# Edge scores as a maximum and a minimum: W1's columns sorted by the sign of W2, self loops as items of the edge stage

## The chip, the core and the metric

The kernel runs on one core of a Trainium2 chip. The metric is device time in microseconds (us), from start to end of one execution. The engines named below are TensorE (PE, matrix products), VectorE (DVE, elementwise), ScalarE (ACT, elementwise with a function and an optional sum), GpSimd (POOL, here mostly the issuer of indirect DMAs) and SyncE (SP, which issues plain DMAs). Each engine runs its own queue in order and waits for the others by semaphores.

## What is computed

Four graph layers are applied to 32 entries of 512 nodes with 256 features. Layers 0 and 3 are of one kind and hold the costly part:

```python
pre_u = jnp.einsum('bud,dk->buk', h_t, W1[:d])
pre_v = jnp.einsum('bvd,dk->bvk', h_t, W1[d:])
hidden = jax.nn.relu(pre_u[:, :, None, :] + pre_v[:, None, :, :] + b1)
S = jax.nn.sigmoid(jnp.einsum('buvk,ko->buvo', hidden, W2)[..., 0] + b2[0])
a_t = jnp.einsum('buv,bud->bvd', S * A_a, h_t)
m_t = jnp.einsum('uv,bud->bvd', A_m, h_t) * h_t
z_t = beta1 * h_t + beta2 * (a_t @ Wa + ba) + beta3 * (m_t @ Wm + bm)   # per entry
```

`A_a` and `A_m` are both the adjacency `adj` (512 x 512), which is nonzero at about 1.6% of its places and on the whole diagonal. The score `S` is therefore needed only where `adj` has an edge. Layer 1 is `z + relu(adj z W^T + b)`; layer 2 is an attention whose logits are `f1[i] + f1[j]`, with a leaky relu, plus `adj`, and a softmax over all 512 nodes.

## The kernel before

**Lists of edges.** `Counts` (L177) counts on the chip how many edges each node has. Eight places per node (`OWN`) are filled from its own edges; what is over goes into four "panels" of 128 lines. If there are more than fit, the register `excess` sends the program into `dense_path`; else `sparse_path` runs. With four blocks of 128 nodes the 32 own items and 4 panels make `ITEMS` = 36 items: an item holds one edge for each of 128 partitions. `Edges.build` makes the indices: `iv` (the row to fetch for the other end), `iu` (for the panels, the row of the first end) and `cell` (where the score goes).

**Groups.** Four entries (`NB`) form a group; there are eight groups, and each passes layer 0 (`g0`) and layer 3 (`g3`), so sixteen edge stages run. `pre` (L583) makes, for each entry of a group and each block of 128 nodes, the products with both halves of W1, adds b1 to the first (L596, DVE), copies the second (L597, ACT), and writes both to a table in HBM (`table`, L604, SP). It also makes the score of the node with itself (L599, L600).

**The edge stage** is `edges` (L649). For each item it fetches 128 rows of the table by an indirect DMA on POOL (L646), 1024 wide (four entries of 256), and adds the first end, `mine` (L731, DVE). `mine` is a plain load on SP (L692) for own items and a gather for the panels. Then relu times W2, summed over 256: in half of the steps, and in all steps of the first and of the last group (`spare`), one 1024-wide DVE instruction (L739) and four summing ACT instructions (L717); in the others four DVE instructions of 256 with an accumulator (L747). Every four items an exponential (L614, ACT), two DVE operations (L618, L619) and a product with the edge's value (L675) make the scores, and POOL scatters them into a dense matrix in HBM (`put`, L639). The scores of the self loops go through the same operations as `own` (`own_1`, L666), at the second and fourth step, and are written to the diagonal by SP (L670). A gather is issued `lead` steps ahead, 3 or, at the ends, 5.

**The rest.** `load` (L772, POOL) brings the finished matrix back as `SA`, once all of the group's puts have landed. `middle_one` does layers 0 to 2 of one entry on PE, with a softmax in between on ACT and DVE (L958 to L964), whose result PE transposes (L1003), and then `pre` for layer 3. `last` does layer 3 of a group.

**The order of the work.** `weave` merges the streams by times written out by hand in units of one group's middle stage (`sparse_path`, L1159 on); a stream is a generator, and each `yield` ends a piece. The middle stages of the groups follow each other; edge stages, the `first` and the `last` of neighbouring groups run beside them. `edge_times` spreads an edge stage's steps over its stretch. The setup, the first group's `pre` and its edge stage come before the first middle stage; the last group's edge stage comes after the last one, beside `last` of the group before, and its own `last_behind` ends the program.

Of the kernel before, what the change touches and what calls it, by code (L numbers as in the profile page):

```python
# [31 lines left out]
LEAD = 3  # L32
LEAD_AT_ENDS = 5
TAIL = 6
EARLY = 20
CELLS = HALF * N
ITEMS = NC * OWN + 2 * PANELS
SPARE = NC // 2 * OWN * P + LINES
GROUP = NB * D
HELD = 12  # L40


def mm(nc, out, pairs):
# [5 lines left out]
class Model:  # L49


    def __init__(self, ctx, tc, a):
        nc = self.nc = tc.nc
        self.tc, self.a = tc, a
        const = self.const = ctx.enter_context(tc.tile_pool(name="const", bufs=1))
        self.ident = const.tile([P, P], F32, name="ident")
        make_identity(nc, self.ident)
        self.adj = const.tile([P, NC, N], F32, name="adj")
        for c in range(NC):
            nc.sync.dma_start(self.adj[:, c, :], a["adj"][c * P : (c + 1) * P, :])  # L60
        self.g0, self.g3 = self.gnn_first("L0_gnn"), self.gnn_first("L3_gnn")

    def rest(self, temp, psum):
# [34 lines left out]
    def gnn_first(self, L):  # L98
        nc, a, const = self.nc, self.a, self.const
        w = {"L": L}  # L100
        w["W1"] = self.load(f"{L}_W1", [P, 2 * DC, D], a[f"{L}_W1"].rearrange("(c p) k -> p c k", p=P))
        w["b1bc"] = self.bcast(f"{L}_b1", D)
        w["W2bc"] = const.tile([P, D], F32, name=f"{L}_W2bc")
        nc.scalar.dma_start(w["W2bc"], a[f"{L}_W2"].rearrange("k o -> (k o)").partition_broadcast(P))
        w["b2"] = self.bcast(f"{L}_b2", 1)
        w["nb2"] = const.tile([P, 1], F32, name=f"{L}_nb2")
        w["bcol"] = const.tile([P, DC, 1], F32, name=f"{L}_bcol")
        if L == "L3_gnn":
            w["bbc"] = const.tile([P, D], F32, name=f"{L}_bbc")
        for key in ("Wa", "Wm"):  # L110
            w[key] = const.tile([P, DC, D], F32, name=f"{L}_{key}")
        return w
# [64 lines left out]
class Counts:  # L177
# [3 lines left out]
    def __init__(self, ctx, m):  # L181
# [4 lines left out]
        with tc.tile_pool(name="c_sb", bufs=2) as sb, tc.tile_pool(name="c_ps", bufs=1, space=PSUM) as ps:  # L186
            ones = sb.tile([P, N], F32, name="c_ones", bufs=1)
            nc.vector.memset(ones, 1.0)
            count = sb.tile([P, NC], F32, name="count", bufs=1)
            there = sb.tile([P, NC], F32, name="c_there", bufs=1)  # L190
            for c in range(NC):
# [13 lines left out]
            nc.tensor.matmul(pc, ones[:, 0:1], self.lines, start=True, stop=True)  # L205
            half = sb.tile([1, 2], F32, name="half")
            nc.vector.tensor_reduce(half, pc.rearrange("p (h c) -> p h c", h=2), AX.X, ALU.add)
            most = sb.tile([1, 1], F32, name="most")
            nc.vector.tensor_reduce(most, half, AX.X, ALU.max)
            nc.vector.tensor_scalar(self.excess, most, float(-LINES), None, ALU.add)  # L210


def item_of(c, k):
# [190 lines left out]
class Group:  # L404
# [3 lines left out]
    def __init__(self, sp, w, name):  # L408
        self.w = w
        self.table = sp.dram.tile([2 * N, GROUP], F32, name=f"table_{name}")  # L410
        self.cells = sp.cells[name[0]]
        self.layer = name[0]
        self.puts = [f"puts_{name}_{q}" for q in range(2)]
        self.written = [[], []]
        self.s = sp.grp.tile([P, ITEMS, NB], F32, name=f"s{name[0]}")
        self.self_s = sp.grp.tile([P, NC, NB], F32, name=f"self_s{name[0]}")


def by_two(t, n=2):
# [3 lines left out]
class Sparse:  # L423
# [98 lines left out]

    def big(self, dtype, n, layer=None):

        self.bigs += 1
        if layer is None:
            layer = 3 if self.bigs <= NC else 0
        return self.act.tile([P, n], dtype, name="big", tag=f"SA{layer}", bufs=NC)

    def setup(self):  # L530


        for w in (self.m.g0, self.m.g3):
            self.nc.vector.tensor_scalar(w["nb2"], w["b2"], -1.0, None, ALU.mult)
        self.zero = self.act.tile([P, GROUP], F32, name="zero", tag="hWa3")
        self.nc.gpsimd.memset(self.zero, 0.0)

        edges = self.built = self.e.build(self.counts, self.adjT, self.lists, self.psum, self.big, self.act)
        for _ in range(NC):
            next(edges)  # L540
            yield
        self.rest = self.m.rest(self.big(F32, 2048), self.psum)
        next(self.rest)
        self.zeros("0")
        yield
        for _ in range(NC + 2 * (OWN // 2 + 1)):
            next(edges)
            yield
# [16 lines left out]

    def setup_rest(self):
        yield from self.rest

# [11 lines left out]
    def pre(self, g, b, hT):  # L582
# [3 lines left out]
        for c in range(NC):  # L586
            cs = slice(c * P, (c + 1) * P)
            if c % 2 == 0:
# [4 lines left out]
            pp = two[c % 2]  # L593
            nc.tensor.matmul(pp, hT[:, 1, cs], w["W1"][:, 1::DC, :], start=False, stop=True)  # L594
            puv = self.small.tile([P, 2, D], F32, name="puv", bufs=3)
            nc.vector.tensor_tensor(puv[:, 0, :], pp[:, 0:D], w["b1bc"], ALU.add)  # L596
            nc.scalar.copy(puv[:, 1, :], pp[:, D:])  # L597
            both = self.small.tile([P, D], F32, name="both", bufs=1)
            nc.vector.tensor_tensor(both, pp[:, D:], puv[:, 0, :], ALU.add)  # L599
            nc.vector.scalar_tensor_tensor(  # L600
                both, both, 0.0, w["W2bc"], ALU.max, ALU.mult, accum_out=g.self_s[:, c, b : b + 1]
            )
            self.settle()
            self.later = lambda c=c, puv=puv: nc.sync.dma_start(rows[:, c, :, b, :], puv)  # L604
            yield
# [44 lines left out]
    def edges(self, g, spare=(), own_tags=()):  # L650
# [11 lines left out]

        def own_1():
            self.sigmoid_of(own)
            diag = self.counts.diag.unsqueeze(2).to_broadcast([P, NC, NB])
            nc.vector.tensor_tensor(g.self_s, g.self_s, diag, ALU.mult)  # L666
            for q in range(2):
                diagonal = g.cells[q][q * HALF : q * HALF + HALF * (N + 1), :]
                diagonal = diagonal.rearrange("(c p a) b -> p c a b", p=P, a=N + 1)[:, :, 0, :]
                self.written(g, q, nc.sync.dma_start(diagonal, g.self_s[:, 2 * q : 2 * q + 2, :]))  # L670

        def run_1(ks):
            self.sigmoid_of(g.s[:, ks, :].rearrange(flat))
# [4 lines left out]
                ready.append((e.half_of(j), e.cell[:, j : j + 1], g.s[:, k, :]))  # L678

        panels = [j for j in e.order if j >= NC * OWN][: len(own_tags)]  # L680

        def fetch(n):
            if n == EARLY:
                for j, tag in zip(panels, own_tags):
                    mine[-j] = self.act.tile([P, GROUP], F32, name="mine_more", tag=tag)
                    self.fetch(mine[-j], g, e.iu[:, j - NC * OWN : j - NC * OWN + 1])
            j = e.order[n]
            c = -j if -j in mine and j >= NC * OWN else j // OWN
            if c not in mine:
                t = self.gath.tile([P, GROUP], F32, name="mine", bufs=3)  # L690
                if c < NC:
# [7 lines left out]
                rows = self.act.tile([P, GROUP], F32, name="rows_more", tag=tag)  # L699
            else:  # L700
                rows = self.gath.tile([P, GROUP], F32, name="rows")
            self.fetch(rows, g, e.iv[:, j : j + 1])
            fetched[n] = rows, t

        def put():
# [4 lines left out]
                self.half = r[0]  # L710
                self.put(g, *r)

        def sums(k, rows):

            for b in range(NB):
                part = rows[:, b * D : (b + 1) * D]
                self.behind(nc.scalar.activation(part, part, AF.Identity, accum_out=g.s[:, k, b : b + 1]))  # L717

        summed = []
        self.half = 1  # L720
# [1 line left out]
            fetch(n)  # L722
            yield

        todo = [(2, lambda: self.exp_of(w, own)), (4, own_1)]
        done = 0
        for k in range(ITEMS):
            for _ in range(2 if spare and len(ready) > 2 else 1):
                put()
            rows, other = fetched.pop(k)  # L730
            self.behind(nc.vector.tensor_tensor(rows, rows, other, ALU.add))  # L731
            if k + lead < ITEMS:
                fetch(k + lead)
            if summed:
                summed.pop(0)()
            if spare or k % 2 == 1 and k < ITEMS - 3:
                by_entry = rows.rearrange("p (b d) -> p b d", b=NB)
                w2 = w["W2bc"].unsqueeze(1).to_broadcast([P, NB, D])
                nc.vector.scalar_tensor_tensor(by_entry, by_entry, 0.0, w2, ALU.max, ALU.mult)  # L739
                summed.append(lambda k=k, rows=rows: sums(k, rows))  # L740
                if spare:
                    summed.pop(0)()
            else:
                for b in range(NB):
                    part = rows[:, b * D : (b + 1) * D]
                    at = g.s[:, k, b : b + 1]
                    nc.vector.scalar_tensor_tensor(part, part, 0.0, w["W2bc"], ALU.max, ALU.mult, accum_out=at)  # L747
            if k % 4 == 3 or k >= ITEMS - 3:
                ks = slice(done, k + 1)
                near = spare or k >= ITEMS - 5  # L750
                todo.append((k + (1 if near else 3), lambda ks=ks: self.exp_of(w, g.s[:, ks, :].rearrange(flat))))
                todo.append((k + (1 if near else 4), lambda ks=ks: run_1(ks)))
                done = k + 1
            while todo and todo[0][0] <= k:
                todo.pop(0)[1]()
            yield
        for _, f in todo:
# [380 lines left out]

def edge_times(ahead, a, b, behind, lead=LEAD):

    step = (b - a) / ITEMS
    first = [ahead + j * min(step, (a - ahead) / lead) for j in range(lead)]
    return first + spread(even(ITEMS), a, b) + spread(even(TAIL), b, behind)


def middle_shares(given):
# [15 lines left out]
def sparse_path(ctx, m, counts, xr, outr, B):  # L1162
# [4 lines left out]
    streams = [  # L1167
        (sp.setup(), spread(even(NC + 1 + NC + 2 * (OWN // 2 + 1) + 1), -0.40, -0.295), ""),
        (sp.setup_behind(), spread(even(2 * (OWN // 2 + 1) + 2 * PANELS + 4), -0.285, -0.16), ""),
        (sp.setup_rest(), spread(even(7), -0.26, -0.20), ""),  # L1170
        (sp.zeros_behind(), spread(even(2), 0.15, 0.2), ""),
    ]
    for t in range(last + 1):
# [276 lines left out]
```

## Time and profile before

| what | value |
|---|---|
| median of the runs | 2977.59 us (2975.59 to 2987.02, 3 runs) |
| the profiled execution, its own time | 2998.45 us |
| its span | 2996.8 us |
| granted PE clock, mean | 0.959 |
| moved by DMA | 677.30 MB |
| first group's edge stage: first add, last add | 90 us, 223 us |
| first load of SA | 229 us |
| last group's edge stage: first add, last add | 2834 us, 2946 us |

Busy times are of one profiled execution. A row of a group of instructions gives line, engine, operation, what it writes from what, shapes, how often; then its busy time in us and the mean duration of one in ns; then the idle time of the engine just before it and what ended most of that. A row of waits gives who waited for what: us in total, times, the longest. A row of windows gives a stretch in us, its length, and the busy us of PE, of PE's weight loads, of DVE, ACT and POOL, each with its number of instructions, then the granted PE clock, the busy share of the DMA engines and GB/s. In the summary the digits are tenths of busy time in 40 equal slices of the span.

### The profile page before, as it was taken

To read this page: it belongs to the slowest core of one execution; us is meant where nothing else is said; L and a number is where in the kernel's file an instruction comes from. 1 tells how busy PE (TensorE), PEld (TensorE's weight loads), DVE (VectorE), ACT (ScalarE), POOL (GpSimd) and SP (SyncE) were. 2 spreads that over 40 slices of the span, in tenths; PEclk is the share of its full clock that TensorE was granted. 3 is DMA by queue.
4 is the path that set the end of the run, shared out by engine and by line. 5 is a ranking of instruction groups with operands and counts; after the bars stand their busy time and mean duration, and the time that the engine had idled before them with its cause. 6 is when DMAs were issued, how large, how long until landed. Compare 5 with 4: busy or idle time off the path is not lost. (4 is left out here: it accounts for less than half of the span.)

```text
span 2996.8 us, 32453 instructions
## 1 busy us (share of the span) xinstructions
PE 2690.0 (90%) x8645; PEld 1613.9 (54%) x8646; DVE 2307.1 (77%) x6035; ACT 1336.8 (45%) x4101; POOL 1555.3 (52%) x1328
## 2 busy tenths in 40 slices
PE   6367787989998999989999899989999899988998
PEld 3134344545664566546664466646565466644666
DVE  6874786889588885988778885888858896783494
ACT  3553454445344443544344443445434453453262
POOL 2662463646445673556536464466735564361183
PEclk9678998999999999999999999999999999999999
DMA  8875657796678867787677866687677866663474
GB/s 268 286 225 169 213 174 221 233 300 203 217 217 269 268 211 227 230 262 254 209 222 247 275 207 230 216 268 253 211 228 236 303 227 197 208 211 102 148 244 150
DMA packets 302143, 677.30 MB, mean 226 GB/s; under 512 B 52608, under 2 KB 170880, under 8 KB 293760
## 3 DMA queue, kind: packets, MB, share of 16 engines
q0 software_dynamic: 122688, 414.40, 42.9%
q1 hardware_dynamic: 160304, 223.52, 23.0%
q10 hardware_dynamic: 18960, 37.24, 3.4%
q8 instruction: 70, 1.15, 0.2%
q14 instruction: 121, 0.99, 0.1%
HBM read 529.02 MB, written 146.01 MB: 225 GB/s over the span
## 5 line engine op out<-in xcount | busy, mean ns | idle before, releaser
L646 POOL DMA_INDIRECT rows<-table,iv x552 | 679.0, 1230 | 795.5 <-DMA table<-puv 262.7
L639 POOL DMA_INDIRECT cells<-s,cell x576 | 697.6, 1211 | 420.6 <-DVE s L675 243.2
L731 DVE TENSOR_TENSOR rows<-rows,mine 128x1024 f32<-128x1024 f32 x552 | 666.4, 1215 | 101.4 <-DMA rows<-table,iv 72.8
L717 ACT ACTIVATE rows<-rows 128x256 f32<-128x256 f32 x1088 | 439.6, 406 | 445.4 <-DVE rows L739 396.6
L46 PE MATMUL pst<-adj,h 128*128 128x512 f32 x1024 | 452.2, 592 | 0.0
L747 DVE SCALAR_TENSOR_TENSOR rows<-rows,L_gnn_W2bc 128x256 f32<-128x256 f32 x1120 | 414.0, 417 | 1.6
L739 DVE SCALAR_TENSOR_TENSOR rows<-rows,L_gnn_W2bc 128x1024 f32<-128x1024 f32 x272 | 329.4, 1213 | 0.4
L46 PEld LDWEIGHTS pst<-adj,h 128*128 128x128 f32 x1024 | 192.8, 190 | 219.9 <-issue 217.6
L46 PE MATMUL pst<-L_gnn_Wa,hT 128*128 128x256 f32 x1024 | 248.8, 393 | 62.9 <-DMA hT<-xT 57.8
L46 PEld LDWEIGHTS pst<-L_gnn_Wa,hT 128*128 128x128 f32 x1024 | 198.9, 199 | 103.0 <-issue 59.2
L46 PE MATMUL pst<-eT,feats 128*128 128x512 f32 x512 | 237.7, 619 | 10.9 <-ACT eT L1004 10.9
L46 PE MATMUL pst<-adjT,zW 128*128 128x512 f32 x512 | 228.2, 599 | 11.6 <-ACT zW L916 9.7
L596 DVE TENSOR_TENSOR puv<-pst,bc_L_gnn_b 128x256 f32<-128x256 f32 x256 | 104.9, 416 | 162.4 <-DMA table<-puv 89.2
L597 ACT COPY puv<-pst 128x256 f32<-128x256 f32 x256 | 93.2, 371 | 288.1 <-DVE puv L596 225.9
L1061 PE MATMUL pst<-hWa,SA 128*128 128x256 f32 x896 | 220.3, 400 | 0.0
L1061 PEld LDWEIGHTS pst<-hWa,SA 128*128 128x128 f32 x896 | 213.8, 328 | 3.7 <-issue 1.7
L717 ACT ACTIVATION_READ_ACCUMULATOR rows<-rows 128x1 f32 x1088 | 204.7, 188 | 0.0
L860 ACT COPY flat<-SA 128x512 f32<-128x512 f32 x128 | 136.7, 1128 | 136.6 <-issue 62.9
L891 PE MATMUL pst<-flat,hWa 128*128 128x512 f32 x448 | 196.8, 592 | 0.0
L592 PE MATMUL pst<-w_L_gnn_W,hT 128*128 128x512 f32 x256 | 141.5, 681 | 53.9 <-ACT hT L579 36.5
L46 PEld LDWEIGHTS pst<-eT,feats 128*128 128x128 f32 x512 | 99.9, 198 | 133.2 <-issue 113.3
L46 PEld LDWEIGHTS pst<-adjT,zW 128*128 128x128 f32 x512 | 96.5, 191 | 133.4 <-issue 114.0
(176 smaller groups left out, 3984.2 us busy)
## 6 DMA issues: line engine op xcount, KB each, us to landing
table<-puv SPq DMA_DIRECT2D x256, 256.0 KB
SA<-cells POOLq DMA_DIRECT2D x64, 1024.0 KB
h<-in_x_dram SPq DMA_DIRECT2D x64, 512.0 KB
mine<-table SPq DMA_DIRECT2D x64, 512.0 KB
hT<-xT SPq DMA_DIRECT2D x36, 512.0 KB
xT<-hT ACTq DMA_DIRECT2D x32, 512.0 KB
x2T<-yT SPq DMA_DIRECT2D x32, 512.0 KB
x2s<-x ACTq DMA_DIRECT2D x64, 256.0 KB
```

The source lines that it names most:

```text
L46: nc.tensor.matmul(out, lhsT, rhs, start=(n == 0), stop=(n == len(pairs) - 1))
L592: nc.tensor.matmul(pp, hT[:, 0, ks], w["W1"][:, 0::DC, :], start=True, stop=False)
L596: nc.vector.tensor_tensor(puv[:, 0, :], pp[:, 0:D], w["b1bc"], ALU.add)
L639: ins = self.nc.gpsimd.indirect_dma_start(out=g.cells[half], out_offset=bass.IndirectOffsetOnAxis(ap=at, axis=0), in_=s, in_offset=None)
L646: self.nc.gpsimd.indirect_dma_start(out=rows, out_offset=None, in_=g.table, in_offset=bass.IndirectOffsetOnAxis(ap=at, axis=0))
L717: self.behind(nc.scalar.activation(part, part, AF.Identity, accum_out=g.s[:, k, b : b + 1]))
L731: self.behind(nc.vector.tensor_tensor(rows, rows, other, ALU.add))
L739: nc.vector.scalar_tensor_tensor(by_entry, by_entry, 0.0, w2, ALU.max, ALU.mult)
L747: nc.vector.scalar_tensor_tensor(part, part, 0.0, w["W2bc"], ALU.max, ALU.mult, accum_out=at)
L860: self.nc.scalar.copy(flat[:, r, :], SA[r][:, :, b])
L891: nc.tensor.matmul(pz, hWa[:, r, cs], flat[:, r, :], start=(r == 0), stop=False)
L1061: self.nc.tensor.matmul(pz[:, k * D : (k + 1) * D], SA[r][:, cs, b], hWa[:, r, :], start=(r + k == 0), stop=(alone and k == 1 and r == NC ...
```

## The change

For a column with weight w, `w * relu(u + v)` equals `max(w v, -w u) + w u` if w is positive and `min(w v, -w u) + w u` if it is negative. So if the tables hold `w v` and `-w u`, an edge needs one maximum over the positive columns, one minimum over the negative ones, a sum, and the subtraction of the sum of the first end's row, which belongs to the node and not to the edge.

- **Ranks** (`ranks`, called in `Counts` ahead of the counting): from W2 as a column the place of each column is made: 112 positive ones first (`SURE`), 112 negative ones next, and the 32 left over (`MIXED`) last. If a sign has fewer than 112 columns, `excess` becomes positive.
- **Sorted W1** (`sorted_W1`, once a layer in the setup): W1 is transposed on PE and multiplied by matrices that hold one scaled entry per column, which sorts and scales it in one product; the same for b1 and W2. The two broadcast loads a layer (b1, W2) are replaced by two loads as columns.
- **`pre`**: L599 and L600 are gone. L596 is split: 224 columns with an accumulator (the sum per node, `less`), and 32 without.
- **`edges`**: 40 steps in place of 36: the four self loops are steps too (`seq`, negative numbers), each with a plain load of its rows on SP, and sums always on ACT. Each step: maximum (4 x 112), minimum (4 x 112), addition (4 x 32), and relu times W2 on 4 x 32. A panel also subtracts its first end, 4 x 224. The sums are on ACT as before, or one DVE reduction over 4 x 256 in place of four accumulating instructions. `less` is subtracted before the exponential: by `own_less` for the self loops, by `less(ks)` for the items. `own_1` runs four steps behind the last self loop. `EARLY` goes from 20 to 24.

```diff
-EARLY = 20
+EARLY = 24
+STEPS = ITEMS + NC
+SURE = 112
+MIXED = D - 2 * SURE
+PLACE = {0: 0, 2: 1, 1: 2, 3: 3}
...
+        nc.scalar.dma_start(w["W2col"], a[f"{L}_W2"].rearrange("(c p) o -> p c o", p=P))
         w["W1"] = self.load(f"{L}_W1", [P, 2 * DC, D], a[f"{L}_W1"].rearrange("(c p) k -> p c k", p=P))
-        w["b1bc"] = self.bcast(f"{L}_b1", D)
-        nc.scalar.dma_start(w["W2bc"], a[f"{L}_W2"].rearrange("k o -> (k o)").partition_broadcast(P))
+        nc.scalar.dma_start(w["b1col"], a[f"{L}_b1"].rearrange("(c p o) -> p c o", p=P, o=1))
...
             nc.vector.memset(ones, 1.0)
+            signs = self.ranks(m, sb, ps, ones)
...
+    def sorted_W1(self, w):
+        nc = self.nc
+        t = self.big(F32, 2048, 0)
+        W1T = t[:, 0 : 2 * N].rearrange("p (c d) -> p c d", c=DC)
+        by_v, by_u = (t[:, k * N : (k + 1) * N].rearrange("p (c d) -> p c d", c=DC) for k in (2, 3))
+        for to, scale in ((by_u, w["su"]), (by_v, w["sv"])):
+            for c in range(DC):
+                nc.vector.tensor_scalar(
+                    to[:, c, :], self.m.upto_D, w["place"][:, c, :], scale[:, c, :], ALU.is_equal, ALU.mult
+                )
+        for c in range(DC):
+            pt = self.psum()
+            for r in range(2 * DC):
+                nc.tensor.transpose(pt[:, r * P : (r + 1) * P], w["W1"][:, r, c * P : (c + 1) * P], self.m.ident)
+            nc.scalar.copy(W1T[:, c, :], pt)
+        for k, to in enumerate((by_u, by_v)):
+            pp = self.psum()
+            for d in range(DC):
+                rs = slice((DC * k + d) * P, (DC * k + d + 1) * P)
+                mm(nc, pp[:, d * D : (d + 1) * D], [(W1T[:, c, rs], to[:, c, :]) for c in range(DC)])
+            nc.scalar.copy(w["W1"][:, DC * k : DC * (k + 1), :], by_two(pp))
...
-            nc.vector.tensor_tensor(puv[:, 0, :], pp[:, 0:D], w["b1bc"], ALU.add)
+            sure = slice(0, 2 * SURE)
+            less = g.less[:, PLACE[c], b : b + 1]
+            nc.vector.scalar_tensor_tensor(
+                puv[:, 0, sure], pp[:, sure], 1.0, w["b1bc"][:, sure], ALU.mult, ALU.add, accum_out=less
+            )
+            nc.vector.tensor_tensor(puv[:, 0, 2 * SURE :], pp[:, 2 * SURE : D], w["b1bc"][:, 2 * SURE :], ALU.add)
             nc.scalar.copy(puv[:, 1, :], pp[:, D:])
-            both = self.small.tile([P, D], F32, name="both", bufs=1)
-            nc.vector.tensor_tensor(both, pp[:, D:], puv[:, 0, :], ALU.add)
-            nc.vector.scalar_tensor_tensor(
-                both, both, 0.0, w["W2bc"], ALU.max, ALU.mult, accum_out=g.self_s[:, c, b : b + 1]
-            )
...
+            if k < 0:
+                nc.sync.dma_start(rows, places[c, 1])
+            else:
+                self.fetch(rows, g, e.iv[:, j : j + 1])
...
-        todo = [(2, lambda: self.exp_of(w, own)), (4, own_1)]
+        todo = [(last_own + 3, own_less), (last_own + 4, own_1)]
...
-            self.behind(nc.vector.tensor_tensor(rows, rows, other, ALU.add))
+            self.behind(nc.vector.tensor_tensor(rows[:, :, ups], rows[:, :, ups], other[:, :, ups], ALU.max))
...
+            nc.vector.tensor_tensor(rows[:, :, downs], rows[:, :, downs], other[:, :, downs], ALU.min)
+            nc.vector.tensor_tensor(rows[:, :, mixed], rows[:, :, mixed], other[:, :, mixed], ALU.add)
+            nc.vector.scalar_tensor_tensor(rows[:, :, mixed], rows[:, :, mixed], 0.0, w2, ALU.max, ALU.mult)
+            if k >= 0 and e.order[k] >= NC * OWN:
+                sure = slice(0, 2 * SURE)
+                nc.vector.tensor_tensor(rows[:, :, sure], rows[:, :, sure], other[:, :, sure], ALU.subtract)
+            to = g.s[:, k, :] if k >= 0 else g.self_s[:, PLACE[-1 - k], :]
-            if spare or k % 2 == 1 and k < ITEMS - 3:
+            if spare or k < 0 or k % 2 == 1 and k < ITEMS - 3:
...
-                for b in range(NB):
-                    part = rows[:, b * D : (b + 1) * D]
-                    at = g.s[:, k, b : b + 1]
-                    nc.vector.scalar_tensor_tensor(part, part, 0.0, w["W2bc"], ALU.max, ALU.mult, accum_out=at)
+                nc.vector.tensor_reduce(to, rows, AX.X, ALU.add)
```

## The prediction

> **What bounds the kernel now.** I read the summary and the slices first, then the waits of TensorE, then windows over the two ends, then the groups.
>
> ```profile
> PE 2690.0 (90%) x8645; PEld 1613.9 (54%) x8646; DVE 2307.1 (77%) x6035; ACT 1336.8 (45%) x4101; POOL 1555.3 (52%) x1328
> ...
> PE   6367787989998999989999899989999899988998
> ...
> DVE  6874786889588885988778885888858896783494
> ```
>
> TensorE (PE) is the bound in the middle, but not at the left end: the first four slices have it at 6, 3, 6, 7 tenths, while VectorE (DVE) is at 6 to 8. PE idles 307 us in all. Its waits:
>
> ```profile
> PE pst L46 <- DMA hT<-xT: 57.8, 4, 25.7
> PE pst L1003 <- DVE ex L964: 51.7, 27, 10.8
> ...
> PE pst L1003 <- DVE cols L963: 29.3, 8, 6.3
> ```
>
> The first row is four waits before 236 us. The other two, 81 us, are the softmax of the middle stage (L958 to L964), held up because DVE has edge work queued before it. The start and the tail by windows:
>
> ```profile
> 90.00:110.00 20.00, 4.09 (x8) 2.44 (x9) 18.67 (x40) 9.47 (x43) 10.76 (x9) 0.50 0.95 367
> 110.00:130.00 20.00, 12.17 (x29) 4.90 (x27) 20.00 (x49) 15.75 (x61) 15.68 (x11) 0.91 0.72 237
> 130.00:150.00 20.00, 0.00 (x0) 0.00 (x0) 20.00 (x47) 9.32 (x44) 14.72 (x12) 0.51 0.70 213
> 150.00:170.00 20.00, 16.52 (x48) 9.66 (x48) 20.00 (x40) 14.30 (x61) 14.60 (x13) 0.89 0.72 216
> ...
> 2834.00:2890.00 56.00, 52.45 (x196) 41.66 (x196) 55.97 (x68) 33.72 (x154) 39.75 (x30) 0.97 0.79 283
> 2890.00:2955.00 65.00, 56.95 (x176) 35.32 (x175) 53.68 (x76) 35.96 (x159) 52.18 (x42) 0.92 0.63 206
> ```
>
> Columns after the length: PE, PE loads, DVE, ACT, POOL. From 90 to 170 us DVE is full (78.7 of 80): this is the first group's edge stage, which must end before the first middle stage may start (its L772 loads run at 229 to 240). From 2834 to 2955, the last group's edge stage, DVE, PE and, with its 0.3 us between DMAs, POOL all have little room. The chain of waits says the same: PE up to 2818, then DVE (L731, L739), then PE.
>
> **The change, part by part.** The rows to price it:
>
> ```profile
> L731 DVE TENSOR_TENSOR rows<-rows,mine 128x1024 f32<-128x1024 f32 x552 | 666.4, 1215 | 101.4 <-DMA rows<-table,iv 72.8
> L717 ACT ACTIVATE rows<-rows 128x256 f32<-128x256 f32 x1088 | 439.6, 406 | 445.4 <-DVE rows L739 396.6
> L747 DVE SCALAR_TENSOR_TENSOR rows<-rows,L_gnn_W2bc 128x256 f32<-128x256 f32 x1120 | 414.0, 417 | 1.6
> L739 DVE SCALAR_TENSOR_TENSOR rows<-rows,L_gnn_W2bc 128x1024 f32<-128x1024 f32 x272 | 329.4, 1213 | 0.4
> L599 DVE TENSOR_TENSOR both<-pst,puv 128x256 f32<-128x256 f32 x256 | 107.3, 419 | 30.7 <-ACT puv L597 21.5 <-ACT flat L860 0.6 <-issue 0.4
> L600 DVE SCALAR_TENSOR_TENSOR both<-both,L_gnn_W2bc 128x256 f32<-128x256 f32 x256 | 107.3, 419 | 2.8
> ```
>
> 256 elements take 0.417 us and 1024 take 1.215, so an instruction costs 0.15 us and 1.04 ns an element. That prices 448 elements (4 x 112) at 0.617, 128 at 0.284, 224 at 0.384, 32 at 0.184, 896 at 1.08. They overlap a little: in the timeline, two independent 1024-wide adds take 2.35 us together. I therefore take 0.07 off each unless the next needs its result.
>
> (a) A step whose sums ACT makes: before, 1.21 + 1.14 = 2.35. After, max 0.54, min 0.54, add 0.28, L739's form 0.21, together 1.57. Saved 0.78.
> (b) A step whose sums DVE makes: before, 1.21 + 4 x 0.42 (L747 with its accumulator read) = 2.89. After, 1.64 and one reduction over 1024. No row shows that reduction; at the bottom it is a 256-wide instruction (0.42), at the top the four accumulating ones (1.68); the nearest row is a 1024-wide pass, 1.14 to 1.21, and I take 1.14: 2.78, saved 0.11.
> (c) Four more steps a group for the self loops, kind (a): 1.57 each. A panel step also subtracts 896 elements, 1.01. The subtractions of `less`, some 11 a group at 128x16, have L675's 0.168, or 0.1 overlapped.
> (d) In `pre`, L599 and L600 go and L596 splits into 224 wide with an accumulator and 32 wide: 1.14 becomes 0.50, 16 times a group: 10.2 saved.
>
> A normal group has 16 steps (a) and 20 (b): 95.4 before; after, 20 x 1.57 + 20 x 2.78 + 4.0 + 1.1 = 92.1; with (d) 13.5 saved. In the first and the last group all steps are (a): 84.6 before, 40 x 1.57 + 5.1 = 67.9 after; with (d) 26.9. All sixteen: 14 x 13.5 + 2 x 26.9 = 243 us of DVE. Without the overlap it is 91; these are the two ends.
>
> A rule speaks against this. The Trainium skill, "VectorE: DVE Perf Modes", The DRAIN you can't avoid, says that each operation is followed by a flush of about its duration less 266 ns, before which the next doesn't start, so that op count should be kept low; its Rules for kernel authors call tensor_reduce the slowest operation, at 1x. By that flush step (a) would go from 4.3 to 2.5 us; but then two 1024-wide adds would need over 3 us to the second's end, and they take 2.35, so the row decides: no flush, 0.78 saved. The 1x is what L731 and L739 already run at, so the reduction gets no surcharge. What remains of the op-count rule is the 0.15 us each, counted above.
>
> (e) ACT: 64 self steps x 4 sums x 0.41 (start to start in the timeline) = 105 us more, on an engine 45% busy: hidden. Without that cover it is 6.6 us a group.
> (f) DMA: 64 plain loads of 512 KB, 34 MB on 677; POOL gets no new instruction. They go on SP's queue and wait there for a `rows` buffer; behind them stand the next `table` writes and the hT and h loads. Costed at nothing because the `mine` loads (L692, also 64 on SP, also issued a lead ahead) never appear as what DVE waited for. Two broadcasts of 128 KB a layer go, two columns come.
> (g) `own_1` moves from step 4 to about step 29 of 40, with its exponential, three 128x16 DVE operations and two SP DMAs of 4 KB. It passes the hT, `mine` and `table` entries of SP; SPq L670 already waits 73.8 us in all. The loads of SA wait for it, but the puts of the last items are later; without those, some 10 steps of slack are left.
> (h) Start, before the branch: `ranks` stands ahead of the counts on DVE and needs the column of L3's W2, fifth on ACT's DMA queue. ACT issued its fifth at 5.2 us; landed at about 7.5, then some 30 small operations at 0.1 to 0.17 and three short PE hops, done at 12; then 2.8 + 0.9 + 1.6 for the counts: 17 against 12.2. **+5**, ends +2 (a landing before 5) and +9 (behind both W1 loads).
> (i) Sorting W1 of L0: 8 transposes (2.2 us at L173's 1.09 per four), 12 matmuls of 256 columns (2.7, at 16 in 3.62), four copies of 0.58, 2.2 us of DVE. Some 8 us in series; the landing of x hides it for the first `pre` (x is issued at 13.0, its transposes start at 21.1), but it stands ahead of the edge lists on DVE and PE: **+3**, ends 0 and +8. L3's sort adds 2.2 us of DVE to 90 to 170.
>
> **The sum**, on the profiled run (span 2996.8 us, its own time 2998.45; the median of the runs is 0.7% less):
> - 0 to 90: +5 +3, and 16 x 0.64 = 10.2 saved in `pre`, of which I count 4, since 30 to 50 us is held by DMA (share 1.01, DVE half idle): +4.
> - 90 to 236: in the full 80 us stand 22 steps, three self steps to come and 10 `pre`: -17.2 + 4.7 - 6.4 + 2.2 = -16.7. Behind 170 DVE waits for PE; I count -2. About -19.
> - 236 to 660: PE waits 38 us before L1003 (summed over the timeline's gaps there); DVE loses 40 x 0.64 + 2 x 3.3 = 32 of some 330. I count -15.
> - 660 to 2640: 32 us of such waits, mostly 1 to 2 us each, which is the latency of the chain: -6. To 2730: 10 us of them: -2.
> - Tail: DVE would give 17, but PE is busy 109 of 121 us there: -7.
> Sum -45: 2953.5, and scaled by the 0.7%, **2933 us**.
>
> **Rivals.**
> 1. **SP turns into a stall** (slower). A self fetch waits on SP for a row buffer. POOL's same wait took 105.9 + 102.5 us in 101 cases, 2.1 us each, longest 26. If SP holds 2.1 us and half reaches PE through late hT or `table`, 64 x 1.05 = +67: 2999. It decides from 0.7 us of PE time per fetch (45 / 64). For it: PE's 57.8 us on hT. Against: `mine`.
> 2. **Hidden.** PE is the bound, the start's cost eats the start's gain, and only the tail gives 7: 2970. For it: 98% PE at 1000 to 1170. Against: DVE full from 90 to 170.
> 3. **More than forecast.** The softmax waits nearly vanish (-60 in place of -23) and the start gives 10 more: 2886.
> 4. The transform does not do what it says: a sign count outside 112 to 144 takes the dense path. The reference's seed gives W2 133 positive values of 256 in both layers (the keys are the same), so both 112s are filled: left out.
>
> **Chances.** Forecast 0.48 (its own range 2905 to 2960), more 0.15, hidden 0.17, SP 0.20. Range for 8 in 10: 2886 to 3000, from the third rival to the first. The runs before spread 0.38%, so 0.5%, 15 us, is about what can be told from no change. Faster by over that: 0.48 + 0.15 and a little of the hidden case, 0.65; within 0.15; slower 0.20.
>
> **What would show it.** DVE busy 2070 to 2215; ACT near 1440; max and min rows at 0.6 us; the reduction at 1.2; first instruction behind the branch at 18 in place of 13; the first SA load some 15 us earlier; the L1003 waits about 55. The forecast is wrong if SP's waits for `rows` come with PE waits on hT or DVE waits on `rows` from `table`, or if DVE waits for ACT's sums at `less`.

## The result, and the profile after

The changed kernel takes 3412.07 us (median; 3405.46 to 3423.3) against 2980.4 in the same session: a ratio of 1.145, with a 95% interval of 1.1407 to 1.1494. Forecast was 2933, with 2886 to 3000 as the range. The time lies far outside it, on the slow side.

The busy times of the page after:

```profile
span 3404.5 us, 33200 instructions
...
PE 2814.4 (83%) x8720; PEld 1679.0 (49%) x8720; DVE 2134.9 (63%) x5789; ACT 1434.6 (42%) x4621; POOL 1364.6 (40%) x1332
...
PE   7567787789978899778987899878997889978978
...
DVE  6745657677466766666576675667746676574363
```

VectorE (DVE) did become lighter, 2135 us in place of 2307, and ACT reached 1435: both as forecast. But no engine is full any more. TensorE (PE) idles 590 us (span less busy) in place of 307, and for nearly the same number of instructions it is busy 124 us longer, at a granted clock of 0.922 in place of 0.959. These two, 283 and 124, are the whole 408 us between the spans.

The loss is spread over the middle. From 800 to 1150 us (columns as in the windows of before):

```profile
800.00:1150.00 350.00, 296.97 (x913) 176.38 (x912) 223.76 (x590) 134.97 (x428) 140.03 (x136) 0.93 0.67 216
```

PE was busy 333.82 of these 350 us before, at a clock of 0.99. The start is not where it went: the first loads of SA run at 210 to 220 us, 19 us sooner than before.

What DVE waits for, in the rows of the costliest groups:

```profile
L867 DVE TENSOR_TENSOR rows<-rows,mine 128x448 f32<-128x448 f32 x608 | 376.1, 619 | 597.2 <-DMA rows<-table,iv 464.9
L862 DVE TENSOR_TENSOR rows<-rows,mine 128x448 f32<-128x448 f32 x608 | 371.0, 616 | 189.4 <-DMA rows<-table,iv 123.4
...
L880 DVE TENSOR_REDUCE s<-rows 128x4 f32<-128x1024 f32 x280 | 336.7, 1204 | 0.5
```

L862 is the maximum, L867 the minimum, L880 the reduction. Each takes what was forecast: 0.617 us for 448 elements, 1.2 for the reduction. New is the idle time: DVE stood 597 us in front of the minimum and 189 in front of the maximum; before, 101 in front of the one addition (L731). In the kernel text the maximum of an item comes first. So its minimum should never have to wait for the gathered rows: they have landed when the maximum starts. It waits because it does not stand behind it. In the compiled list of DVE's instructions the minimum precedes the maximum of its own item in 447 of 640 cases.

In the timeline (start, length, instruction, idle before it and its releaser):

```profile
1532.68 1.21 DVE L880 TENSOR_REDUCE s<-rows 128x4 f32<-128x1024 f32 x1
1533.81 0.27 DVE L869 SCALAR_TENSOR_TENSOR rows<-rows,L_gnn_W2bc 128x128 f32<-128x128 f32 x1
1539.26 0.63 DVE L867 TENSOR_TENSOR rows<-rows,mine 128x448 f32<-128x448 f32 x1 [5.17 <-DMA rows<-table,iv]
1539.80 0.28 DVE L868 TENSOR_TENSOR rows<-rows,mine 128x128 f32<-128x128 f32 x1
1540.12 0.29 DVE L869 SCALAR_TENSOR_TENSOR rows<-rows,L_gnn_W2bc 128x128 f32<-128x128 f32 x1
1540.33 0.68 DVE L940 TENSOR_TENSOR mhT<-pst,hT 128x512 f32<-128x512 f32 x1
```

A minimum stands 5.17 us at the head of DVE's queue for its gather. Behind it stands L940, a product of the middle stage that feeds PE's matmuls. The waits of PE show the same end of it; L1038, L1062 and L1120 are DVE work of the middle stage, and L669 is an ACT copy ahead of `pre`. After, then the like rows of before:

```profile
PE pst L682 <- ACT hT L669: 120.6, 17, 14.9
PE pst L1051 <- DVE hT L1038: 82.2, 22, 11.1
PE pst L1073 <- DVE yT L1062: 52.8, 28, 5.4
...
PE pst L682 <- DVE yT L1120: 35.6, 11, 5.5
```

```profile
PE pst L592 <- ACT hT L579: 36.5, 11, 4.9
...
PE pst L934 <- DVE yT L923: 11.2, 14, 1.6
...
PE pst L912 <- DVE hT L899: 8.2, 6, 2.3
```

### The profile page after: what moved, and what is told of

Its sections match the earlier page's. It is cut to its first block, busy times and chain, and to the rows that moved or that the text cites. A ratio compares the mean times of both kernels' runs of the same rounds, so it can differ in the third digit from the quotient of the medians.

```text
span 3404.5 us, 33200 instructions
## 1 busy us (share of the span) xinstructions
PE 2814.4 (83%) x8720; PEld 1679.0 (49%) x8720; DVE 2134.9 (63%) x5789; ACT 1434.6 (42%) x4621; POOL 1364.6 (40%) x1332
## 5 line engine op out<-in xcount | busy, mean ns | idle before, releaser
L736 POOL DMA_INDIRECT rows<-table,iv x548 | 581.0, 1060 | 1298.3 <-ACT rows L846 298.1
L846 ACT ACTIVATE rows<-rows 128x256 f32<-128x256 f32 x1320 | 532.4, 406 | 544.2 <-DVE rows L862 321.1
L867 DVE TENSOR_TENSOR rows<-rows,mine 128x448 f32<-128x448 f32 x608 | 376.1, 619 | 597.2 <-DMA rows<-table,iv 464.9
L729 POOL DMA_INDIRECT cells<-s,cell x576 | 615.8, 1069 | 295.4 <-issue 139.1
L862 DVE TENSOR_TENSOR rows<-rows,mine 128x448 f32<-128x448 f32 x608 | 371.0, 616 | 189.4 <-DMA rows<-table,iv 123.4
L880 DVE TENSOR_REDUCE s<-rows 128x4 f32<-128x1024 f32 x280 | 336.7, 1204 | 0.5
L846 ACT ACTIVATION_READ_ACCUMULATOR rows<-rows 128x1 f32 x1320 | 249.9, 189 | 5.2 <-issue 5.2
L1051 PE MATMUL pst<-WT,hT 128*128 128x256 f32 x512 | 153.6, 465 | 91.4 <-DVE hT L1038 82.2
L1073 PE MATMUL pst<-WT,yT 128*128 128x257 f32 x512 | 137.5, 418 | 60.9 <-DVE yT L1062 52.8
L1051 PEld LDWEIGHTS pst<-WT,hT 128*128 128x128 f32 x512 | 120.1, 239 | 134.0 <-DVE hT L1038 78.6
L688 DVE SCALAR_TENSOR_TENSOR puv<-pst,L_gnn_b1bc 128x224 f32<-128x224 f32 x256 | 98.4, 384 | 132.1 <-PE pst L684 75.0
```

The costliest lines, as they stand in the source:

```text
L729: ins = self.nc.gpsimd.indirect_dma_start(out=g.cells[half], out_offset=bass.IndirectOffsetOnAxis(ap=at, axis=0), in_=s, in_offset=None)
L736: self.nc.gpsimd.indirect_dma_start(out=rows, out_offset=None, in_=g.table, in_offset=bass.IndirectOffsetOnAxis(ap=at, axis=0))
L862: self.behind(nc.vector.tensor_tensor(rows[:, :, ups], rows[:, :, ups], other[:, :, ups], ALU.max))
L867: nc.vector.tensor_tensor(rows[:, :, downs], rows[:, :, downs], other[:, :, downs], ALU.min)
L880: nc.vector.tensor_reduce(to, rows, AX.X, ALU.add)
L1051: nc.tensor.matmul(pw[:, at], zT[:, d, cs], m.WT_1[:, d, :], start=(d + k == 0), stop=(d * k == 1))
```

## The experiments

**Why would the minimum run ahead?** The text of a kernel here is not its final order: the instructions are scheduled anew per engine, and what depends on nothing may be moved forward. `behind` adds an order that carries no data: an instruction of an edge stage may not come before a mark of the middle stage. The kernel before wrapped its one addition in it, and everything else in the step used the addition's result. The change wraps the maximum alone. Minimum and mixed addition write other columns, so neither depends on the maximum.

Three theories were put against each other: this one of the **order**; **SP**, whose queue holds the middle's loads behind the self fetches; and the **lead**, gathers issued too late for 40 denser steps.

```diff
-            nc.vector.tensor_tensor(rows[:, :, downs], rows[:, :, downs], other[:, :, downs], ALU.min)
-            nc.vector.tensor_tensor(rows[:, :, mixed], rows[:, :, mixed], other[:, :, mixed], ALU.add)
+            self.behind(nc.vector.tensor_tensor(rows[:, :, downs], rows[:, :, downs], other[:, :, downs], ALU.min))
+            self.behind(nc.vector.tensor_tensor(rows[:, :, mixed], rows[:, :, mixed], other[:, :, mixed], ALU.add))
```

> The minimum and the addition of the mixed columns are also ordered behind the middle stage, as the maximum is. Order theory (the minimum, which nothing orders, stands in DVE's queue in front of the maximum of its own item and waits there for the gather): DVE's waits on rows from the table fall from about 660 us to under 200, PE idles about 300 us in place of 585, time 2920 to 2990. SP theory (the self fetches on SP's queue hold the loads of the middle stage): time stays above 3300. Lead theory (the gathers are issued too late for the shorter steps): time stays above 3300.

Measured: 3041.78 us, ratio to before 1.0192 (1.0152 to 1.0231). Two changed lines take back 370 of the 432 us, where the other two theories had the time above 3300. DVE's waits on `rows` are down to 168 us and PE's idle time to 327, of which the copy at L669 has 35.7. No minimum stands in front of its maximum any more, and the rows say so:

```profile
L862 DVE TENSOR_TENSOR rows<-rows,mine 128x448 f32<-128x448 f32 x608 | 376.1, 619 | 194.7 <-DMA rows<-table,iv 151.3 <-issue 17.2 <-DMA rows<-table 13.8
L867 DVE TENSOR_TENSOR rows<-rows,mine 128x448 f32<-128x448 f32 x608 | 371.5, 611 | 0.0
```

The wait at the minimum is gone, not moved: the maximum's is what it was. But the time is above the expected 2990, so something else is left.

Then the same fault alone, put into the kernel before: the addition cut in three, with the second and third piece free, or held.

```diff
-            self.behind(nc.vector.tensor_tensor(rows, rows, other, ALU.add))
+            self.behind(nc.vector.tensor_tensor(to[0], to[0], by[0], ALU.add))
...
+            for i in (1, 2):
+                nc.vector.tensor_tensor(to[i], to[i], by[i], ALU.add)
```

> The kernel before, with its addition of 1024 cut into 112, 112 and 32 columns of each entry; only the first piece is ordered behind the middle stage. Nothing else of the change. Order theory: slower by 4 to 14%, 3100 to 3400, with DVE waiting for rows at the free pieces. SP theory and lead theory: only the two more DVE instructions a step count, about 0.15 us each, 576 times: 0 to 3% slower, 2980 to 3070.

> As the split of the kernel before, but all three pieces are ordered behind the middle stage. All theories: 0 to 3% slower than before, 2980 to 3070; only if the mere number of DVE instructions did the harm would it be as slow as the one with free pieces.

Measured: free 3185.93, ratio 1.0665 (1.0626 to 1.0703); held 3040.15, 1.0181 (1.0137 to 1.0224). With equal work on DVE (2373 and 2376 us busy), the order alone is worth 146 us, in a kernel with no maximum, no self step and no sorted W1. In the free one DVE waits at a free piece (L740), in the held one at the first piece (L734), and less. The free one, then the held one:

```profile
DVE rows L740 <- DMA rows<-table,iv: 258.8, 108, 11.6
...
DVE rows L734 <- DMA rows<-table,iv: 51.0, 28, 12.5
```

```profile
DVE rows L734 <- DMA rows<-table,iv: 47.2, 26, 13.0
```

The held one has a price too: 1.8% for 69 us more of DVE's work (2376.3 against 2307.1), from the cutting alone.

Does it take a large piece? The next one holds the minimum and leaves only the 32-column addition (L868, 0.28 us) free.

> The minimum is ordered behind the middle stage as the maximum is; the addition of the 32 mixed columns is left free, as in the changed kernel. Order theory: one free piece is enough, since it is the first instruction to touch the gathered rows: DVE waits at the addition, over 300 us, and the time is 3200 to 3420. If only the minimum did the harm: 3030 to 3060.

Measured: 3369.86, ratio 1.132 (1.1301 to 1.1339).

```profile
L867 DVE TENSOR_TENSOR rows<-rows,mine 128x448 f32<-128x448 f32 x608 | 370.2, 610 | 0.0
...
L868 DVE TENSOR_TENSOR rows<-rows,mine 128x128 f32<-128x128 f32 x608 | 172.5, 286 | 616.6 <-DMA rows<-table,iv 547.2 <-DMA mine<-table,iu 58.7 <-DMA rows<-table 4.5
```

The wait goes to whichever piece is free, and a piece of 0.28 us does nearly the harm of the whole (1.132 against 1.145): 172 us of work cost 617 us of waiting. Two rivals were tried on the changed kernel as it is:

```diff
-LEAD = 3
+LEAD = 4
-        self.act, self.small, self.gath = pool("act", 1), pool("small", 2), pool("gath", 5)
+        self.act, self.small, self.gath = pool("act", 1), pool("small", 2), pool("gath", 6)
-        tags = [None] * 5 + list(spare)
+        tags = [None] * 6 + list(spare)
```

> The changed kernel with its order as it is, but gathers issued four steps ahead in place of three, and six row buffers in place of five. Lead theory: most of the loss goes, 2950 to 3100. Order theory: the minimum moves ahead with the schedule, so only a part goes, 3200 to 3400. SP theory: no change, 3380 to 3430.

```diff
-            puv = self.small.tile([P, 2, D], F32, name="puv", bufs=3)
+            puv = self.small.tile([P, 2, D], F32, name="puv", bufs=5)
```

> The changed kernel with its order as it is and five puv buffers. Order theory: the wait on gathers stays at the minimum, over 400 us; 3340 to 3420. If the table writes were the main cause: under 3200.

Measured: 3391.26, ratio 1.1351 (1.1308 to 1.1394), and 3434.06, 1.1485 (1.1434 to 1.1536). Neither a longer lead nor more buffers cure the order: DVE's waits at the minimum are 507 and 523 us. The lead takes back one of the 14.5 percentage points, the small end of what the order theory allowed; 3391 lies in the range of the SP theory too, so it is the mended order that decides against SP. The five buffers gain nothing here (two runs, 14 us above the range of the order theory, interval overlapping that of the changed kernel): their gain, below, needs the right order first.

**The 2% that are left.** With the order mended DVE has 189 us less work than before (2118.1 against 2307.1), and the kernel is still slower. Its longest waits:

```profile
DVE rows L862 <- DMA rows<-table,iv: 154.3, 68, 13.2
DVE puv L688 <- DMA table<-puv: 117.0, 37, 10.4
```

Before, these were 72.8 and 89.2:

```profile
DVE puv L596 <- DMA table<-puv: 89.2, 39, 5.9
DVE rows L731 <- DMA rows<-table,iv: 72.8, 49, 12.4
```

At `puv` DVE waits, in `pre`, for one of the three `puv` buffers, which comes free when its write to the table has landed. The held split of the kernel before lost as much by the cutting alone (1.0181); how much of that price lies in these 2% too, no run tells. Four runs on the mended kernel:

```diff
-                nc.sync.dma_start(rows, places[c, 1])
+                nc.gpsimd.dma_start(rows, places[c, 1])
```

> All of the changed kernel's pieces held as before, and the self loops' rows loaded by POOL's queue in place of SP's. SP theory for the 2% that is left (self fetches hold SP, the table writes come late, DVE waits at puv): DVE's wait on table<-puv falls from 117 us to under 90, time 2960 to 3010. Lead theory (the 40 denser steps give each gather less time): no gain, 3030 to 3060.

> All pieces held, and five puv buffers in place of three, so that DVE need not wait at puv for the table writes. SP theory: DVE's 117 us at puv go to under 30, PE's waits for yT before the products of pre (31 us) with them, time 2950 to 3000. Lead theory: 3020 to 3050.

> All pieces held, gathers four steps ahead in place of three, six row buffers in place of five. Lead theory: DVE's wait on rows from the table falls from 154 us to under 80, time 2970 to 3010. SP theory: 3020 to 3050.

> All pieces held, and the self loops left out: 36 steps, no self fetches on SP, their scores are zero and so the result lacks them. This prices the four self steps a group. If they are what eats the gain: 2930 to 2980. If the remaining loss is elsewhere: 3000 to 3040.

| run | us | ratio to before (95%) | DVE waits at puv / at rows, us |
|---|---|---|---|
| mended order | 3041.78 | 1.0192 (1.0152 to 1.0231) | 117 / 154 |
| self fetches on POOL | 3042.77 | 1.0167 (1.0132 to 1.0203) | 118 / 145 |
| five puv buffers | 2972.71 | 0.9931 (0.9903 to 0.9959) | not among the longest / 189 |
| lead 4, six row buffers | 3005.28 | 1.0062 (1.0039 to 1.0085) | 133 / 110 |
| without self loops | 2999.88 | 1.0039 (1.0023 to 1.0056) | 66 / 123 |

SP is not the place: with the self fetches on POOL's queue nothing changes. That also speaks against my slow rival. The buffers are: two more take 2.4 to 2.6% off (against the second row, of the same session, and the first), and this version is 0.7% faster than before. Its time is the one that the SP theory named, but what that theory had right is the wait at `puv`, not SP. The lead helps too, by 1.0 to 1.3%, though DVE's wait on rows fell to 110 us and not under the expected 80. The self steps cost 1.3 to 1.5%; at 3000 us that run lies on the lower edge of the range for a loss that lies elsewhere. In the timelines a table write is issued 0.1 us after its ACT copy in the mean, in this version as before. So DVE waits for the landing, not for SP. How the buffers' gain reaches PE is not shown: the waits for yT that were to go with it stayed (31.0 us at L684, 40.1 with five buffers).

Is this a gain that the kernel before would have had as well?

> The kernel before with four puv buffers in place of three, nothing else (five do not fit beside its other tiles). If the buffers alone made the gain, it is 1 to 2% faster than before, 2930 to 2960. If they only undo what the change added: 2965 to 2990.

> All pieces held and four puv buffers: the like of the kernel before with four. Between the version with three, 3042, and with five, 2973: 2970 to 3010; DVE's wait on table<-puv under 60 us in place of 117.

Measured: 2986.96, ratio 0.9995 (0.9983 to 1.0006), and 2998.49, 1.0029 (1.0011 to 1.0048). The fourth buffer gives the kernel before nothing and the mended one 1.6%, so the shortage is of the change's making. The wait itself is no measure of it: in the kernel before, the fourth buffer took DVE's wait at puv from 89.2 to 15.4 us, and its wait for gathered rows rose from 72.8 to 122.6. With five, a longer lead was tried on top:

> All pieces held, five puv buffers, gathers four steps ahead with the five row buffers as they are. If the wait on rows (189 us of DVE in the version with five puv buffers) is a matter of the lead: 2935 to 2965. If the row buffers come free too late for an earlier gather: 2965 to 2990.

Measured: 2973.16, 0.994 (0.9917 to 0.9962): nothing more. The wait on rows is still 174 us; without a sixth row buffer, for which there is no room beside five of `puv`, the lead does not help.

Two runs took the remaining parts of the change apart, and one tried to lower the price of the self steps:

```diff
             nc.scalar.copy(puv[:, 1, :], pp[:, D:])
+            both = self.small.tile([P, D + 1], F32, name="both", bufs=1)
+            nc.vector.tensor_tensor(both[:, 0:D], pp[:, D:], puv[:, 0, :], ALU.add)
+            nc.vector.scalar_tensor_tensor(
+                both[:, 0:D], both[:, 0:D], 0.0, self.m.upto_D, ALU.max, ALU.mult, accum_out=both[:, D : D + 1]
+            )
```

> All pieces held, three puv buffers, and the two removed DVE instructions of pre put back as dead work (256 wide each, 16 times a group, about 165 us of DVE in all). If their time covered the landing of the table writes: the wait at puv falls from 117 us to about 90 and the time stays or falls, 3010 to 3045. If not, DVE's work is simply added: 3060 to 3120.

> All pieces held, five puv buffers, the self loops left out (36 steps, their scores zero, the result lacks them). If the losses of self steps (1.5% with three buffers) and of puv (2.6%) add up: 2925 to 2940. If both act through the same wait at puv: 2950 to 2975.

```diff
-            if spare or k < 0 or k % 2 == 1 and k < ITEMS - 3:
+            if spare or k >= 0 and k % 2 == 1 and k < ITEMS - 3:
```

> All pieces held, five puv buffers, and the self loops' sums made by one DVE reduction in place of four ACT sums, but for the first and last group. If the row buffer held for ACT is what costs: POOL's wait for ACT before gathers falls from about 200 us, and the time is 2940 to 2965. If it is the four more steps themselves (DVE, DMA): 2970 to 2995, as 1.14 us of DVE a step comes on top.

With the two dead instructions in `pre`: 3105.86, ratio 1.0456 (1.0421 to 1.049). The wait at puv does fall, from 117 to 76 us, so their time had covered part of the landing. But the time goes up 2.6%, for 178 us more of DVE's work: the cover was worth less than the work. That `pre` got lighter is a real gain.

Without self loops and with five buffers: 2898.99, ratio 0.974 (0.9724 to 0.9757), below both ranges. The self steps thus cost 1.9% here and the missing buffers 3.0%: the two losses add up, or to a little more than their sum. As the buffers gain as much without the self steps, it is not the self steps that made them short.

With the self sums on DVE: 2951.91, ratio 0.9926 (0.9898 to 0.9955), the same as with five buffers within the intervals. In microseconds this lies in the range of the row buffer theory, but the kernel before ran at 2978.31 in that session and at 2986.6 in the other. POOL's wait for ACT's sums before a gather does fall, from 160 us with five buffers to 73, but DVE has 57 us more to do, and nothing is won. A self step costs 0.6 to 0.9 us of the kernel's time (39 to 57 us over 64 steps), less than its 1.57 us of DVE. How much of it is due to DVE, to the row buffers, to 34 MB of DMA or to 6.6 us of ACT a group was not told apart.

## Why the prediction was wrong

- **The step that failed is (a)**, and (b) with it. It added up four DVE instructions as one block in the place of the old addition, and so put their wait for the gathered rows at nothing. The durations of the new pieces were right (0.619 and 0.286 us against 0.617 and 0.284). Their place was not: only the first carries the order behind the middle stage. DVE stood idle 597 us in front of the minimum. The prediction priced DVE by its work and the self loops' loads by their queue, and never asked what each new instruction waits for when nothing orders it. It had the question's wording before it (`self.behind` around the maximum alone in the diff), and the row that showed the danger: L731 was what waited for the gathers (72.8 us), because it was the first to touch them. After the change every item has three such first touches. Order is worth 12.6 of the 14.5 points (1.145 to 1.0192).
- **(d) and the buffers.** Saving two DVE instructions in `pre` is worth 2.6%, as a part of the work. The `puv` buffers behind it were not counted; this missing term is 2.4 to 2.6% with five buffers in place of three. That they are short because `pre` got shorter fits the wait that fell when its work was put back (117 to 76 us), but was not tested with five buffers, so this cause is argued and not shown.
- **(c), (e) and (f)**, the self steps: priced at 6.3 us of DVE a group inside the sum. At the sum's own rate, 45 us of time for 243 of DVE, that is about 19 us for all sixteen; they cost 1.3 to 1.9%, 39 to 57 us. The sign that was named for a stall of SP, DVE's waits on `rows` from `table`, did appear in the changed kernel (60.6 us at the maximum), but it fell to 13.8 with the order mended, and moving the fetches to POOL gained nothing.
- **(h)**: the first instruction behind the branch is at 15.1 us in place of 13.0, so +2, the lower end of the estimate. (i) has no figure of its own. The first load of SA was forecast 15 us sooner and is 19 sooner.
- **The flush rule**, which was laid aside for the row: in the timeline of the changed kernel two 448-wide instructions of 0.61 us start 0.54 apart. A flush that grows with the duration is not seen. The prediction gave the rule without its limit: the section it names in the Trainium skill, "VectorE: DVE Perf Modes", The DRAIN you can't avoid, also says that a next operation which is not held starts earlier.
- **The softmax** waits of PE (81 us) were to fall to about 55: 96 in the changed kernel, 45 in the mended one, 67 in the one with the self fetches on POOL. A good part of the gain was there once the order was.
- **The sum** of -45 us: with order and buffers mended it is 0.69% faster (about 20 us), less than half of it, and without the self loops' steps, which the result needs, 2.6% (about 77 us). The sign was right only with both mended, and the rate at which DVE's time turns into the kernel's, 45 us for 243, looks too low: 178 us put back into `pre` cost 64 us or more, and 69 us in the held split about 50. The kernel as written does not show the gain.

**A misreading in (b).** The prediction took the four L747 at their mean length, 0.417 us each. They overlap, as the timeline of before shows (start, length):

```profile
311.38 0.42 DVE L747 SCALAR_TENSOR_TENSOR rows<-rows,L_gnn_W2bc 128x256 f32<-128x256 f32 x1
...
311.72 0.42 DVE L747 SCALAR_TENSOR_TENSOR rows<-rows,L_gnn_W2bc 128x256 f32<-128x256 f32 x1
...
312.07 0.42 DVE L747 SCALAR_TENSOR_TENSOR rows<-rows,L_gnn_W2bc 128x256 f32<-128x256 f32 x1
...
312.41 0.42 DVE L747 SCALAR_TENSOR_TENSOR rows<-rows,L_gnn_W2bc 128x256 f32<-128x256 f32 x1
```

At 0.35 us from start to start the old step is about 1.14 + 4 x 0.35 = 2.5 us, not 2.89. The new one, with pieces that start 0.54, 0.54, 0.20 and 0.20 us apart and a reduction of 1.13, is 2.6. These steps save nothing. An estimate from these figures: some 50 of the forecast 243 us of DVE. Measured were 172, and 189 in the mended kernel, inside the stated ends, of which 91 is given without its working.

## What to carry to other kernels

When one instruction is cut into several that write different parts, an order without data that was tied to the first does not pass on to the others: tie it to each, and look in the compiled order whether any of them ran ahead. On an engine that works in order, price a new instruction by what it waits for at the place where it will stand, not by its duration. Count a wait by what it moves in the kernel's time: a wait for a buffer can vanish and come back at the next instruction. When a change makes the stages of a pipeline shorter, count the buffers between them again.

## What the hardware showed that was not expected

PE's idle time costs more than itself. PE has 22 idle gaps of 3 to 11 us before and 53 after; the granted clock fell from 0.959 to 0.922, and PE was busy 124 us longer for almost the same instructions (8720 against 8645). The clocks alone would turn 2690 us into 2798, an estimate: 108 of the 124. The mended kernel, with the same 8720 instructions as the changed one, has a clock of 0.956 and PE busy for 2703.9 us. The Trainium skill's "TensorE: Matmul & The Clock Gate", Part 1: The HAM clock gate, says that the clock is halved after an idle window of about 3.4 us and needs about as long a stretch of activity to recover. The traces agree: their records of the clock have it at half for 247 us in 34 stretches before and for 535 us in 78 after, and between whole and half they show nothing. The clock of 0.936 at a ratio of 1.0665 fits too, though no run here isolates the 3.4 us.

POOL's gathers got quicker wherever DVE's long addition was cut: 1230 ns each before, 1137 in the held split, 1092 in the mended kernel, 1060 in the changed one. That DVE idled more is not reason enough, for in the held split it was busier than before (78% of the span against 77%). The profile's times on POOL are rough, and what the reason is stays open.
